# A recurrent mixing loop whose value rows are spread by DMA instead of by TensorE, with the orders of VectorE and ScalarE written out

## The chip, the cores and the metric

The kernel runs on one core of a Trainium2 chip. The core has TensorE (PE, matrix products, with its weight loads shown apart as PEld), VectorE (DVE), ScalarE (ACT), GpSimd (POOL) and SyncE (SP, which here only issues transfers). SBUF is the working memory of 128 partitions, PSUM the memory that TensorE writes to. Each engine has its own queue of instructions, and engines wait for each other by semaphores.

The metric is the device time of one execution in microseconds. The profile is taken from one execution of the program.

## The reference

Four layers run one after the other on an input of 8 batches, 256 rows and 512 channels, all in float32: a cross-attention layer with combined weights, a recurrent mixing layer, a pair of attentions with an MLP, and a non-local block. The change lies in the second layer. Cut to what matters, for each batch (S = 256 positions, 32 heads of 16 channels):

```
xa = layernorm(x); sx = shifted(xa) - xa
xw, xk, xv, xr, xg = xa + sx * (maa_* + low-rank mixes of xa and sx)
w = exp(-exp(time_decay + tanh(xw @ decay_w1) @ decay_w2))
r, k, v = xr @ Wr.T, xk @ Wk.T, xv @ Wv.T      # each head: 16 channels
g = silu(xg @ Wg.T)
for each position l, each head:
    a     = k_l[:, None] * v_l[None, :]         # 16 x 16
    out_l = r_l @ (faaaa * a + s)
    s     = a + w_l[:, None] * s
y = group_norm(out);  x = x + (y * g) @ Wo.T
xc = layernorm(x); sxc = shifted(xc) - xc       # channel mix
x = x + sigmoid(xr2 @ fWr.T) * (relu(xk2 @ fWk.T) ** 2 @ fWv.T)
```

The state of a head is 16 x 16 numbers, each of which follows a recurrence over the 256 positions: multiply by w of its row, add k of its row times v of its column.

## The kernel before

The program is written with a scheduling layer. Whatever is traced as an instruction carries its data dependences; a planner then orders the instructions of each engine by its own estimate of when they are ready, except where the program pins them. Two ways of pinning occur. `manual_schedule(engines=...)` keeps the named engines in the order of the program; `keep_in_program_order` does so for one instruction. The middle stage (class Middle, which holds the mixing layer and the two attentions) runs with PE pinned. DVE, ACT, POOL and SP are ordered by the planner there, apart from single pinned instructions.

**Layout.** Channels lie on partitions, 128 at a time (ct = 0 to 3), positions along the free dimension. For one batch, one ct and one half hf, a step of the loop handles 8 heads x 16 rows (128 partitions) x 8 value columns x 256 positions. So there are 8 x 4 x 2 = 64 steps, eight to a batch.

**One step** (functions spread, states and gather):

- `spread` (line 902): the value rows must stand on every partition of their head. Eight matmuls with a constant 0/1 matrix esel copy 32-partition groups of v to the PSUM tile vb (128 x 8 x 255). vb is 8 KB a partition, four of PSUM's eight banks, and has one buffer.
- `states`: on every second step ACT computes exp(-w) broadcast four times (w4, lines 912 and 913). DVE writes the initial state in column 0 of vb (line 921), multiplies vb by k in place in two halves (line 924), and runs two scans (line 928) over vb and w4. POOL multiplies each scan's result by r (line 933).
- `gather` (line 945): PE sums over the rows of the heads with the constant gsel into yp; on every second step DVE adds the bonus term hv (line 951).

**The filler.** All the rest of the layer is given as a list `steps + after` of (time, function): the projections k, v, r, g of a later batch, the mixes (`mixed`, line 777 on DVE), layernorms (`norm`, `normed`, `cm_norm`, `cm_normed`, `ln_stats` with its Ln and Exp on ACT at lines 60 and 61), the group norm (`head_norm`, `head_norm2`, `gated`, `gate`), `out_proj` and the channel mix (`cm_mix`, `cm_k`, `cm_r`, `cm_v`). The time is in steps; an item of batch b stands at 8 (b - 1) plus its time. So 19.1, the gate, falls on step 3.1 of a set of eight steps; 19.5, the output projection, on 3.5; 21, cm_norm, on 5.0; 7.1 is the second half of r. `fill.until(t)` traces all items up to t. Within a step the program traces: states(n), the filler up to n + 0.95, gather(n - 1), the filler up to n + 0.99 (the mixed items, which stand at .97), spread(n + 1). That order is PE's order.

**Banks.** Products of the filler go to PSUM tiles of tag mm, of which there are three during the loop. Most are emptied by ACT, those of mixed, bonus, out_proj, cm_v and partly g by DVE.

**Weights.** Eight weight matrices a batch pass through five buffers; each is loaded (line 1640, two transfers from SP) when the buffer's former user is behind it in the list. In the first layer's stage, which runs before with PE, DVE, ACT and POOL pinned, line 501 stores the result of a batch.

Of the kernel before, what the change touches and what calls it, by code (L numbers as in the profile page):

```python
# [10 lines left out]
F32 = mybir.dt.float32  # L11
AF = mybir.ActivationFunctionType
ALU = mybir.AluOpType
# [3 lines left out]
P = 128  # L17
B, S, D = 8, 256, 512
ST = S // P
CT = D // P  # L20
# [73 lines left out]
def rows_of(halves):  # L94

    return [halves[k // 2][:, k % 2, :] for k in range(CT)]
# [20 lines left out]
def stage_l0(g, pools):  # L117
# [492 lines left out]

    "bones": (P,), "bmean": (P,), "cmean": (P,),

    "esel": (4, P), "gsel": (4, 32),
    "bfa": (CT, P),
}
NMB, NMC = (
# [5 lines left out]
class Middle:  # L622
# [62 lines left out]
    def plan(self):  # L685
        g, cp, wpool = self.g, self.cp, self.wpool
        nc, I = g.nc, g.I
        HS, NG = 16, 4
        w1, w2, w2g, d1, d2, s0, bones, bmean, cmean, esel, gsel, bfa = self.c.values()

        class sm:
            tile = staticmethod(lambda *a, **k: self.sm.tile(*a, **k))
# [18 lines left out]
        bufs = [4]  # L711
# [6 lines left out]


        t_ = {}  # L720

        def fetch(b, tag, bufs):
            x = t_[tag, b] = wk.tile([P, ST, D], F32, tag=tag, name=tag, bufs=bufs)
            nc.sync.dma_start(out=x, in_=g.x1[b])

        def norm(b):
            t_["st", b] = ln_stats(g, sm, t_["xi", b])
# [79 lines left out]
                    nc.scalar.activation(w[:, ct, :], wp[:, j, :], AF.Exp, bias=g.pv("time_decay", ct))  # L807

        def load(b, W):
            t_[W, b] = rows_of(g.weight(wpool, I["l1" + W + "T"], name=W))  # L810

        def proj(b, W, src, c2):
            pp = mm("proj")
# [76 lines left out]
            nc.vector.tensor_tensor(xb[:, st, :], xb[:, st, :], op, ALU.add)  # L890


        vbs, rss, w4s, yps = {}, {}, {}, {}

        def spread(b, ct, hf):

            v_ = t_["v", b]
            vb = vbs[b, ct, hf] = ps.tile([P, NG, 2, S], F32, tag="vb", name="vb", bufs=1)
            for j in range(2):
                for n in range(NG):  # L900
                    r = slice(32 * n, 32 * n + 32)
                    nc.tensor.matmul(  # L902
                        vb[:, n, j, 1:S], lhsT=esel[r, 2 * hf + j, :], rhs=v_[r, ct, 0 : S - 1],
                        start=True, stop=True,
                    )

        def states(b, ct, hf):


            if hf == 0:  # L910
                w4 = w4s[b, ct] = wk.tile([P, 4, S], F32, tag="w4", name="w4")
                nc.scalar.memzero(w4[:, :, 0:1])
                nc.scalar.activation(
                    w4[:, :, 1:S], t_["w", b][:, ct : ct + 1, 0 : S - 1].to_broadcast([P, 4, S - 1]),
                    AF.Exp, scale=-1.0,
                )
            w4 = w4s[b, ct]
            kb = t_["k", b][:, ct : ct + 1, 0 : S - 1].to_broadcast([P, 4, S - 1])
            rb = t_["r", b][:, ct : ct + 1, :].to_broadcast([P, 4, S])
            vb = vbs.pop((b, ct, hf)).rearrange("p n j l -> p (n j) l")  # L920
            nc.vector.tensor_copy(vb[:, :, 0], s0[:, b, ct, hf])
            for n2 in range(2):
                h = vb[:, 4 * n2 : 4 * n2 + 4, 1:S]
                nc.vector.tensor_tensor(h, h, kb, ALU.mult)  # L924
            rss[b, ct, hf] = []
            for n2 in range(2):
                a = wk.tile([P, 4, S], F32, tag="a", name="a", bufs=6)
                nc.vector.tensor_tensor_scan(  # L928
                    a.rearrange("p n l -> p (n l)"), w4.rearrange("p n l -> p (n l)"),
                    vb[:, 4 * n2 : 4 * n2 + 4, :].rearrange("p n l -> p (n l)"), 0.0, ALU.mult, ALU.add,  # L930
                )
                rs = wk.tile([P, 4, S], F32, tag="a", name="rs", bufs=6)
                nc.gpsimd.tensor_tensor(rs, a, rb, ALU.mult)  # L933
                rss[b, ct, hf].append(rs)

        def gather(b, ct, hf):
            if hf == 0:
                yps[b, ct] = ps.tile([P, S], F32, tag="y", name="yp", bufs=1)
                if ct % 2 == 0:
                    t_["y", b, ct // 2] = wk.tile([P, 2, S], F32, tag="y", name="y", bufs=2)  # L940
            yp = yps[b, ct]
            rs2 = rss.pop((b, ct, hf))
            for j in range(2):
                for n in range(NG):
                    nc.tensor.matmul(
                        yp[32 * n : 32 * n + 32, :], lhsT=gsel[:, 2 * hf + j, :],
                        rhs=rs2[n // 2][:, 2 * (n % 2) + j, :],
                        start=(hf == 0 and j == 0), stop=(hf == 1 and j == 1),
                    )
            if hf == 1:  # L950
                nc.vector.tensor_tensor(
                    t_["y", b, ct // 2][:, ct % 2, :], yp, t_["hv", b][:, ct, :], ALU.add
                )
# [42 lines left out]

        def store(b):
            g.x2[b] = g.dram([P, ST, D], f"x2_{b}")
            nc.sync.dma_start(out=g.x2[b], in_=t_.pop(("xo", b)))


        HD, NH = 32, 4
        runs = [(pre, b) for pre in ("a_", "c_") for b in range(B)]

        pin = lambda ins: self.tc.keep_in_program_order(ins)

        def at_fetch(i):
            pre, b = runs[i]
# [170 lines left out]
        def values(i, ct):  # L1179
# [21 lines left out]
            (1.97, mixed, 0, *wk_), (2.97, mixed, 1, *wk_), (3.97, mixed, 0, *vr_), (4.97, mixed, 1, *vr_),  # L1201
            (5.97, mixed, 0, *g_), (6.97, mixed, 1, *g_),
            (4.2, decay), (4.1, kvrg, "k", 0), (5.2, decay2), (5.1, kvrg, "k", 1),
            (5.5, kvrg, "v", 0), (6.1, kvrg, "v", 1), (6.3, kvrg, "r", 0), (7.1, kvrg, "r", 1),
            (8.5, kvrg, "g", 0), (10.3, kvrg, "g", 1), (10.7, bonus),
            (13.4, head_norm, 0), (14.3, head_norm2, 0), (14.9, gated, 0), (15.8, gate, 0),
            (15, fetch, "xo", 2), (17.2, head_norm, 1), (18.05, head_norm2, 1), (18.6, gated, 1), (19.1, gate, 1),
# [18 lines left out]
        fill = self.fill = Filler()  # L1226
# [28 lines left out]
        for pre, i, q, kv, o in (("a_", 0, "w_qkv", "w_qkv", "w_ao"), ("c_", B, "w_q", "w_kv", "w_co")):  # L1255
            c = D if q == kv else 0
# [8 lines left out]
        for lo, hi, fn in spans:  # L1265
            free.sort()
            at = free.pop(0)
# [4 lines left out]
        def loop(psums):  # L1272
            every = [(b, ct, hf) for b in range(B) for ct in range(CT) for hf in range(2)]
            bufs[0] = 3
            fill.until(-0.001)
            spread(*every[0])
            for n, at in enumerate(every):
                states(*at)
                fill.until(n + 0.95)
                if n:  # L1280
                    gather(*every[n - 1])
                fill.until(n + 0.99)
                if n + 1 < len(every):
                    spread(*every[n + 1])
            gather(*every[-1])

            psums.close()
            self.ps = psums.enter_context(self.tc.tile_pool(name="atp", bufs=8, space=PSUM))
            bufs[0] = 8
            every = [(i, ct) for i in range(2 * B) for ct in range(CT)]  # L1290
            stream = [(i, ct, h2) for i, ct in every for h2 in range(2)]
            for n in range(-1, len(every)):
                fill.until(A0 + n + 0.05)
                if n + 1 < len(every):
                    scores(*every[n + 1])
                for k in (2 * n + 2, 2 * n + 3):
                    if k < len(stream):
                        masked(*stream[k])
                        exps(*stream[k])
                    if 0 < k <= len(stream):  # L1300
                        divided(*stream[k - 1])
                    if 1 < k:
                        turn(*stream[k - 2])
                fill.until(A0 + n + 0.95)
                if n > 1:
                    values(*every[n - 2])
                fill.until(A0 + n + 0.99)
            values(*every[-2])
            fill.until(A0 + len(every) + 0.99)
            values(*every[-1])  # L1310
            fill.until(999)
            psums.close()
            return t_["ln", 2 * B]
# [366 lines left out]
def host_layout(i):  # L1680

    f = np.float32
# [19 lines left out]
        a["l1" + nm + "T"] = T(L1[nm])  # L1702

    vo = np.arange(D).reshape(CT, 8, 16).transpose(0, 2, 1).reshape(-1)
    for nm in ("Wv", "Wg"):
        a["l1" + nm + "T"] = a["l1" + nm + "T"][:, vo]
    a["l1WoT"] = a["l1WoT"][vo]
    for nm in ("maa_w1", "decay_w1", "decay_w2"):
        a[nm] = L1[nm]
    w2 = L1["maa_w2"]  # L1710
    a["maa_w2p"], a["maa_w2g"] = w2[0:4].reshape(P, D), w2[4]

    a["sh"] = np.ascontiguousarray(c[:, 0:2].reshape(B, 2, CT, P).transpose(3, 1, 2, 0))

    s0 = c[:, 2:18].reshape(B, CT, P, 4, 2, 2).transpose(2, 0, 1, 4, 3, 5)
    a["s0"] = s0.reshape(P, B, CT, 2, 8)
    hs, th = np.arange(P) // 16, np.arange(P) % 8
    a["bones"] = (hs[:, None] == th[None, :]).astype(f)
    a["bmean"] = (th[:, None] == th[None, :]).astype(f) / 16
    a["cmean"] = np.eye(P, dtype=f) - a["bmean"]  # L1720
    t4 = np.arange(P) // 8 % 4
    a["esel"] = np.stack([((t4 == t)[:, None] & (th[:, None] == hs[None, :])) for t in range(4)], 1).astype(f)
    a["gsel"] = np.stack([((t4 == t)[None, :32] & (hs[:, None] == th[None, :32])) for t in range(4)], 1).astype(f)
    for nm in ("w_qkv", "w_ao", "w_q", "w_kv", "w_co", "w1", "w2"):
        a[nm] = L2[nm]
    a["thwT"] = T(L3["theta_w"])
# [1 line left out]
    a["wwT"] = T(L3["w_w"])  # L1728
    pv = {
        "gn_w": L1["gn_w"][vo], "gn_b": L1["gn_b"][vo],  # L1730
        "bo": L0["bo"], "rwb": L0["r_w_bias"], "faaaa": L1["faaaa"],
        "a_ln_s": L2["ln1_s"], "a_ln_b": L2["ln1_b"], "c_ln_s": L2["ln2_s"], "c_ln_b": L2["ln2_b"],
        "m_ln_s": L2["ln3_s"], "m_ln_b": L2["ln3_b"],
        "a_bq": L2["b_qkv"][0:D], "a_bk": L2["b_qkv"][D : 2 * D],
# [34 lines left out]
```

## Time and profile before

| what | us |
|---|---|
| median of 3 runs (3416.64 to 3420.81) | 3419.39 |
| the profiled execution | 3402.09 |
| its span in the profile | 3400.3 |
| mixing loop, first spread to last scan | 1375 to 2162 |

The profile's first part gives the busy time of each engine. Its rows by line give a group's count, its busy time, the mean of one in ns, and the idle time of the engine just before the group with what ended it. The table of stretches gives busy time per engine in a window and the mean granted clock of PE. The timeline lists instructions in order of time; in brackets stands how long the engine had been idle and what released it. "issue" is waiting for nothing that the profile shows.

### The profile page before, as it was taken

The numbers are of one execution on the slowest core, as the hardware profiler recorded it, in microseconds if no ns is written. First come the engines' busy times: TensorE is split into PE (matmuls) and PEld (weight loads), VectorE is DVE, ScalarE is ACT, GpSimd is POOL, SyncE is SP. The second block draws the span as 40 slices with busy tenths as digits, with TensorE's granted clock in tenths as the row PEclk, the third lists the DMA queues.
The fourth block names the chain that finished last, engine by engine and source line by source line (L and its number), as shares of the span: only waits on it lengthen the run. The fifth ranks groups of instructions, "written<-read, shape, count | busy, mean of one in ns | idle before, by whom it ended". The sixth has DMA issues, their size and how long they took to land. (4 is left out here: it accounts for less than half of the span.)

```text
span 3400.3 us, 68714 instructions
## 1 busy us (share of the span) xinstructions
PE 3186.7 (94%) x26496; PEld 2274.7 (67%) x26496; DVE 2408.6 (71%) x4175; ACT 1590.1 (47%) x3983; POOL 1663.7 (49%) x1776
## 2 busy tenths in 40 slices
PE   8999999999999997889999998899999997899999
PEld 6677777777777764656666655555555553799996
DVE  5666666666666664787787887667888886777771
ACT  4555555555555553224334333565656664323223
POOL 7533333333333232456656655443444443788872
PEclk9999999999999998889999999899999997999999
DMA  8666565656657542312323323267687776400002
GB/s 280 226 203 196 187 195 187 205 179 197 205 185 223 174 128 69 112 52 91 106 93 106 99 101 101 100 218 243 237 279 265 266 260 235 164 1 1 1 13 87
DMA packets 273141, 533.08 MB, mean 157 GB/s; under 512 B 25056, under 2 KB 147312, under 8 KB 268720
## 3 DMA queue, kind: packets, MB, share of 16 engines
q1 hardware_dynamic: 251616, 456.48, 41.6%
q10 hardware_dynamic: 20528, 70.39, 5.5%
q8 instruction: 211, 3.46, 0.4%
q0 software_dynamic: 672, 1.81, 0.2%
q14 instruction: 114, 0.93, 0.1%
HBM read 411.15 MB, written 117.44 MB: 155 GB/s over the span
## 5 line engine op out<-in xcount | busy, mean ns | idle before, releaser
L391 POOL TENSOR_SCALAR pe<-pe,rinv 128x512 f32<-128x512 f32 x256 | 176.9, 691 | 608.4 <-DVE rinv L390 605.8
L368 DVE TENSOR_REDUCE nmax<-sp 128x2 f32<-128x1024 f32 x256 | 309.1, 1217 | 176.6 <-PE sp L363 176.6
L933 POOL TENSOR_TENSOR rs<-a,r 128x1024 f32<-128x1024 f32 x128 | 302.7, 2380 | 254.4 <-DVE a L928 223.2
L1161 POOL TENSOR_SCALAR pe<-pe,rinv 128x256 f32<-128x256 f32 x512 | 235.3, 478 | 307.2 <-DVE rinv L1159 301.0
L377 ACT ACTIVATE pe<-sp,nmax 128x512 f32<-128x512 f32 x512 | 347.1, 683 | 11.2
L1151 ACT ACTIVATE pe<-pe,nmax 128x256 f32<-128x256 f32 x512 | 255.0, 499 | 200.5 <-DVE nmax L1142 197.7
L403 DVE STREAM_TRANSPOSE pt<-pe 128x1024 f32<-128x1024 f32 x256 | 312.8, 1231 | 24.2 <-POOL pe L391 15.3
L432 PE MATMUL av<-pt,vr 32*64 32x256 f32 x8192 | 263.8, 390 | 37.6 <-issue 28.9
L928 DVE TENSOR_TENSOR_SCAN a<-w,vb 128x1024 f32<-128x1024 f32 x128 | 287.4, 2276 | 4.8
L432 PEld LDWEIGHTS av<-pt,vr 32*64 32x64 f32 x8192 | 211.0, 136 | 102.8 <-issue 58.2
L363 PE MATMUL sp<-k,q 64*64 64x512 f32 x2048 | 265.8, 611 | 7.3 <-ACT pe L377 7.3
L373 ACT ACTIVATE nmax<-nmax 128x2 f32<-128x2 f32 x256 | 51.8, 202 | 397.8 <-DVE nmax L368 397.6
L303 PEld LDWEIGHTS gp<-t,ws 128*128 128x128 f32 x1512 | 184.8, 192 | 31.2 <-ACT pe L396 11.4
L303 PE MATMUL gp<-t,ws 128*128 128x128 f32 x1512 | 202.2, 277 | 2.5 <-POOL ws L289 1.4
L396 ACT ACTIVATE pe<-pe,rinv 128x512 f32<-128x512 f32 x256 | 182.6, 729 | 41.4 <-DVE rinv L390 41.4
L924 DVE TENSOR_TENSOR vb<-vb,k 128x1020 f32<-128x1020 f32 x128 | 157.2, 1228 | 4.4
L1171 DVE STREAM_TRANSPOSE dt<-pe 128x1024 f32<-128x1024 f32 x128 | 155.6, 1215 | 3.7 <-POOL pe L1161 3.7
L1447 ACT ACTIVATE h<-h,pvec 128x256 f32<-128x256 f32 x124 | 55.9, 500 | 201.6 <-DVE h L1416 164.6
L902 PE MATMUL vb<-v,mconstc 32*128 32x255 f32 x1024 | 98.9, 441 | 54.8 <-DVE a L928 54.0
L390 DVE RECIPROCAL rinv<-ssum 128x2 f32<-128x2 f32 x256 | 41.2, 161 | 146.8 <-ACT pe L377 146.8
L455 PEld LDWEIGHTS op<-av_sb,wo 128*128 128x128 f32 x512 | 92.2, 190 | 55.4 <-issue 27.5
L455 PE MATMUL op<-av_sb,wo 128*128 128x256 f32 x512 | 126.3, 390 | 2.1 <-issue 2.1
(311 smaller groups left out, 7537.7 us busy)
## 6 DMA issues: line engine op xcount, KB each, us to landing
pt<-dt ACTq DMA_DIRECT2D x128, 512.0 KB, 3.9
pt<-pt SPq DMA_DIRECT2D x512, 128.0 KB, 3.6
ws<-sqk SPq DMA_DIRECT2D x110, 512.0 KB, 4.8
wqk<-in_wqk_dram SPq DMA_DIRECT2D x70, 512.0 KB, 5.5
vr<-v SPq DMA_DIRECT2D x128, 256.0 KB, 4.7
ws<-sv SPq DMA_DIRECT2D x56, 512.0 KB, 4.9
wv<-in_wv_dram SPq DMA_DIRECT2D x36, 512.0 KB, 5.1
v<-vT SPq DMA_DIRECT2D x64, 256.0 KB, 2.5
```

Source lines behind the costliest of these rows:

```text
L303: nc.tensor.matmul(out[:, hf * P : (hf + 1) * P], lhsT=w[n](hf, k), rhs=a[n](hf, k), start=k == 0, stop=k == ST - 1,)
L363: nc.tensor.matmul(sp[a * 64 : (a + 1) * 64, h, :], lhsT=qs[b, 2 * un + a][r, ic], rhs=ks[b, 2 * un + a][r, :], start=True, stop=True,)
L368: nc.vector.tensor_reduce(nmax, sp, AX.X, ALU.max, negate=True)
L377: nc.scalar.activation(pe[:, h, :], sp[:, h, :], AF.Exp, bias=nmax[:, h : h + 1], scale=1.0 / DH ** 0.5, accum_out=ssum[:, h : h + 1],)
L396: nc.scalar.mul(pe[:, 1, :], pe[:, 1, :], rinv[:, 1:2])
L403: nc.vector.transpose(pts[b, un][:, it], pe)
L432: nc.tensor.matmul(av[r][h * DH : (h + 1) * DH], lhsT=vr[rows_, kb, h * DH : (h + 1) * DH], rhs=pt[rows_, :, h, 32 * kb : 32 * kb + 32], s ...
L455: nc.tensor.matmul(op, lhsT=wo[0][:, p % 4, mt * P : (mt + 1) * P], rhs=avs[b, p][:, c], start=p % 4 == 0, stop=p % 4 == 3,)
L928: nc.vector.tensor_tensor_scan(a.rearrange("p n l -> p (n l)"), w4.rearrange("p n l -> p (n l)"), vb[:, 4 * n2 : 4 * n2 + 4, :].rearrange( ...
L933: nc.gpsimd.tensor_tensor(rs, a, rb, ALU.mult)
L1151: pin(nc.scalar.activation(pe[:, r, :], pe[:, r, :], AF.Exp, bias=nmax[:, r : r + 1], scale=-1.0, accum_out=ssum[:, r : r + 1],))
L1161: pin(nc.gpsimd.tensor_scalar(pe[:, r, :], pe[:, r, :], rinv[:, r : r + 1], 1.0, ALU.mult, ALU.mult))
```

## The change

The value rows no longer pass through PE. v of a batch is stored to DRAM in two halves (`v_store`, at 5.8 and 6.45 in the list). For a step, `spread` issues eight transfers from DRAM to an SBUF tile vl (two buffers), one for each head residue h: the eight rows of a head's half are read 16 times, to the partitions h, h + 8, h + 16 and so on. `lift` copies vl to PSUM (vb) with two ScalarE copies of 128 x 1020 and, on every second step, computes w4. spread runs two steps ahead; lift(n + 1) is traced at n + 0.5.

In the loop, DVE and ACT join PE in the written order. The transfers of the loop (weights, fetches, stores, spreads) are pinned on SP. To let a head's rows lie at stride 8, the columns of Wr, Wk, the decay and faaaa are permuted on the host as those of v and g already were; esel is gone, and gsel, bones and s0 follow the new layout. The scratch for software DMA is set to 4096 bytes.

```diff
-            nc.sync.dma_start(out=x, in_=g.x1[b])
+            pin(nc.sync.dma_start(out=x, in_=g.x1[b]))
...
-            t_[W, b] = rows_of(g.weight(wpool, I["l1" + W + "T"], name=W))
+            t_[W, b] = rows_of(g.weight(wpool, I["l1" + W + "T"], name=W, pin=pin))
...
+        def v_store(b, c2):
+            if c2 == 0:
+                t_["vd", b] = g.dram([P, CT, S], f"v{b}")
+            c = slice(2 * c2, 2 * c2 + 2)
+            pin(nc.sync.dma_start(out=t_["vd", b][:, c, :], in_=t_["v", b][:, c, :]))
 
         def spread(b, ct, hf):
 
-            v_ = t_["v", b]
-            vb = vbs[b, ct, hf] = ps.tile([P, NG, 2, S], F32, tag="vb", name="vb", bufs=1)
-            for j in range(2):
-                for n in range(NG):
-                    r = slice(32 * n, 32 * n + 32)
-                    nc.tensor.matmul(
-                        vb[:, n, j, 1:S], lhsT=esel[r, 2 * hf + j, :], rhs=v_[r, ct, 0 : S - 1],
-                        start=True, stop=True,
-                    )
-
-        def states(b, ct, hf):
+            rows = t_["vd", b].rearrange("(g f h) c s -> h f c g s", f=2, h=2 * NG)
+            vl = vls[b, ct, hf] = wk.tile([P, 2 * NG, S], F32, tag="vl", name="vl", bufs=2)
+            for h in range(2 * NG):
+                pin(nc.sync.dma_start(
+                    out=vl[h :: 2 * NG, :, 1:S], in_=rows[h, hf, ct, :, 0 : S - 1].partition_broadcast(HS)
+                ))
+
+        def lift(b, ct, hf):
 
+            vl = vls.pop((b, ct, hf))
+            vb = vbs[b, ct, hf] = ps.tile([P, 2 * NG, S], F32, tag="vb", name="vb", bufs=1)
+            for n2 in range(2):
+                h = slice(NG * n2, NG * n2 + NG)
+                nc.scalar.copy(vb[:, h, 1:S], vl[:, h, 1:S])
             if hf == 0:
                 w4 = w4s[b, ct] = wk.tile([P, 4, S], F32, tag="w4", name="w4")
...
+            pin(nc.sync.dma_start(out=g.x2[b], in_=t_.pop(("xo", b))))
...
+            (5.5, kvrg, "v", 0), (6.1, kvrg, "v", 1), (5.8, v_store, 0), (6.45, v_store, 1), (6.3, kvrg, "r", 0), (7.1, kvrg, "r", 1),
...
+            fill.until(-1.45)
+            spread(*every[0])
+            spread(*every[1])
             fill.until(-0.001)
-            spread(*every[0])
-            for n, at in enumerate(every):
-                states(*at)
-                fill.until(n + 0.95)
-                if n:
-                    gather(*every[n - 1])
-                fill.until(n + 0.99)
-                if n + 1 < len(every):
-                    spread(*every[n + 1])
+            lift(*every[0])
+            with self.tc.manual_schedule(engines={getattr(mybir.EngineType, e) for e in ("PE", "DVE", "Activation")}):
+                for n, at in enumerate(every):
+                    states(*at)
+                    if n + 2 < len(every):
+                        spread(*every[n + 2])
+                    fill.until(n + 0.5)
+                    if n + 1 < len(every):
+                        lift(*every[n + 1])
+                    fill.until(n + 0.95)
+                    if n:
+                        gather(*every[n - 1])
+                    fill.until(n + 0.99)
             gather(*every[-1])
...
-    for nm in ("Wv", "Wg"):
+    for nm in ("Wr", "Wk", "Wv", "Wg"):
         a["l1" + nm + "T"] = a["l1" + nm + "T"][:, vo]
...
-    nc = _bacc.Bacc("TRN2", target_bir_lowering=False, num_devices=1)
+    nc = _bacc.Bacc("TRN2", target_bir_lowering=False, num_devices=1, dynamic_dma_scratch_size=4096)
```

More of the change, by code (lines that the diff above doesn't have):

```diff
@@ L611 @@
     "bones": (P,), "bmean": (P,), "cmean": (P,),
-    "esel": (4, P), "gsel": (4, 32),
+    "gsel": (4, 32),
     "bfa": (CT, P),
@@ L688, in plan @@
         HS, NG = 16, 4
-        w1, w2, w2g, d1, d2, s0, bones, bmean, cmean, esel, gsel, bfa = self.c.values()
+        w1, w2, w2g, d1, d2, s0, bones, bmean, cmean, gsel, bfa = self.c.values()
         class sm:
@@ L720, in plan @@
         t_ = {}
+        pin = lambda ins: self.tc.keep_in_program_order(ins)
         def fetch(b, tag, bufs):
             x = t_[tag, b] = wk.tile([P, ST, D], F32, tag=tag, name=tag, bufs=bufs)
-            nc.sync.dma_start(out=x, in_=g.x1[b])
+            pin(nc.sync.dma_start(out=x, in_=g.x1[b]))
         def norm(b):
@@ L890, in out_proj @@
             nc.vector.tensor_tensor(xb[:, st, :], xb[:, st, :], op, ALU.add)
-        vbs, rss, w4s, yps = {}, {}, {}, {}
-        def spread(b, ct, hf):
-            v_ = t_["v", b]
-            vb = vbs[b, ct, hf] = ps.tile([P, NG, 2, S], F32, tag="vb", name="vb", bufs=1)
-            for j in range(2):
-                for n in range(NG):
-                    r = slice(32 * n, 32 * n + 32)
-                    nc.tensor.matmul(
-                        vb[:, n, j, 1:S], lhsT=esel[r, 2 * hf + j, :], rhs=v_[r, ct, 0 : S - 1],
-                        start=True, stop=True,
-                    )
-        def states(b, ct, hf):
+        vls, vbs, rss, w4s, yps = {}, {}, {}, {}, {}
+        def v_store(b, c2):
[3 more added lines that the diff above has]
+            pin(nc.sync.dma_start(out=t_["vd", b][:, c, :], in_=t_["v", b][:, c, :]))
+        def spread(b, ct, hf):
+            rows = t_["vd", b].rearrange("(g f h) c s -> h f c g s", f=2, h=2 * NG)
[10 more added lines that the diff above has]
+                nc.scalar.copy(vb[:, h, 1:S], vl[:, h, 1:S])
             if hf == 0:
@@ L916, in states @@
                 )
+        def states(b, ct, hf):
             w4 = w4s[b, ct]
@@ L919, in states @@
             rb = t_["r", b][:, ct : ct + 1, :].to_broadcast([P, 4, S])
-            vb = vbs.pop((b, ct, hf)).rearrange("p n j l -> p (n j) l")
+            vb = vbs.pop((b, ct, hf))
             nc.vector.tensor_copy(vb[:, :, 0], s0[:, b, ct, hf])
             for n2 in range(2):
-                h = vb[:, 4 * n2 : 4 * n2 + 4, 1:S]
+                h = vb[:, NG * n2 : NG * n2 + NG, 1:S]
                 nc.vector.tensor_tensor(h, h, kb, ALU.mult)
@@ L929, in states @@
                     a.rearrange("p n l -> p (n l)"), w4.rearrange("p n l -> p (n l)"),
-                    vb[:, 4 * n2 : 4 * n2 + 4, :].rearrange("p n l -> p (n l)"), 0.0, ALU.mult, ALU.add,
+                    vb[:, NG * n2 : NG * n2 + NG, :].rearrange("p n l -> p (n l)"), 0.0, ALU.mult, ALU.add,
                 )
@@ L945, in gather @@
                     nc.tensor.matmul(
-                        yp[32 * n : 32 * n + 32, :], lhsT=gsel[:, 2 * hf + j, :],
+                        yp[32 * n : 32 * n + 32, :], lhsT=gsel[:, 2 * j + hf, :],
                         rhs=rs2[n // 2][:, 2 * (n % 2) + j, :],
@@ L998, in store @@
             g.x2[b] = g.dram([P, ST, D], f"x2_{b}")
-            nc.sync.dma_start(out=g.x2[b], in_=t_.pop(("xo", b)))
+            pin(nc.sync.dma_start(out=g.x2[b], in_=t_.pop(("xo", b))))
         HD, NH = 32, 4
         runs = [(pre, b) for pre in ("a_", "c_") for b in range(B)]
-        pin = lambda ins: self.tc.keep_in_program_order(ins)
         def at_fetch(i):
@@ L1203, in plan @@
             (4.2, decay), (4.1, kvrg, "k", 0), (5.2, decay2), (5.1, kvrg, "k", 1),
-            (5.5, kvrg, "v", 0), (6.1, kvrg, "v", 1), (6.3, kvrg, "r", 0), (7.1, kvrg, "r", 1),
+            (5.5, kvrg, "v", 0), (6.1, kvrg, "v", 1), (5.8, v_store, 0), (6.45, v_store, 1), (6.3, kvrg, "r", 0), (7.1, kvrg, "r", 1),
             (8.5, kvrg, "g", 0), (10.3, kvrg, "g", 1), (10.7, bonus),
@@ L1709, in host_layout @@
         a[nm] = L1[nm]
+    a["decay_w2"] = a["decay_w2"][:, vo]
     w2 = L1["maa_w2"]
@@ L1713, in host_layout @@
     a["sh"] = np.ascontiguousarray(c[:, 0:2].reshape(B, 2, CT, P).transpose(3, 1, 2, 0))
-    s0 = c[:, 2:18].reshape(B, CT, P, 4, 2, 2).transpose(2, 0, 1, 4, 3, 5)
+    s0 = c[:, 2:18].reshape(B, CT, 8, 16, 4, 2, 2).transpose(3, 2, 0, 1, 6, 4, 5)
     a["s0"] = s0.reshape(P, B, CT, 2, 8)
-    hs, th = np.arange(P) // 16, np.arange(P) % 8
-    a["bones"] = (hs[:, None] == th[None, :]).astype(f)
+    th = np.arange(P) % 8
+    a["bones"] = (th[:, None] == th[None, :]).astype(f)
     a["bmean"] = (th[:, None] == th[None, :]).astype(f) / 16
@@ L1721, in host_layout @@
     t4 = np.arange(P) // 8 % 4
-    a["esel"] = np.stack([((t4 == t)[:, None] & (th[:, None] == hs[None, :])) for t in range(4)], 1).astype(f)
-    a["gsel"] = np.stack([((t4 == t)[None, :32] & (hs[:, None] == th[None, :32])) for t in range(4)], 1).astype(f)
+    a["gsel"] = np.stack([((t4 == t)[None, :32] & (th[:, None] == th[None, :32])) for t in range(4)], 1).astype(f)
     for nm in ("w_qkv", "w_ao", "w_q", "w_kv", "w_co", "w1", "w2"):
@@ L1730, in host_layout @@
         "gn_w": L1["gn_w"][vo], "gn_b": L1["gn_b"][vo],
-        "bo": L0["bo"], "rwb": L0["r_w_bias"], "faaaa": L1["faaaa"],
+        "bo": L0["bo"], "rwb": L0["r_w_bias"], "faaaa": L1["faaaa"].reshape(-1)[vo], "time_decay": L1["time_decay"][vo],
         "a_ln_s": L2["ln1_s"], "a_ln_b": L2["ln1_b"], "c_ln_s": L2["ln2_s"], "c_ln_b": L2["ln2_b"],
```

## The prediction

> **What bounds the kernel now.** The page's busy line and its rows name the engines of the whole run; a table by stretches then picks out the mixing loop (1375 to 2162 us), the only stage that the change touches; the timeline gives its order.
>
> ```profile
> PE 3186.7 (94%) x26496; PEld 2274.7 (67%) x26496; DVE 2408.6 (71%) x4175; ACT 1590.1 (47%) x3983; POOL 1663.7 (49%) x1776
> ...
> L902 PE MATMUL vb<-v,mconstc 32*128 32x255 f32 x1024 | 98.9, 441 | 54.8 <-DVE a L928 54.0
> ```
> The spread matmuls (L902) keep PE busy for 98.9 us, 1.55 us a step over 64 steps.
>
> ```profile
> 1571.00:1669.00 98.00, 93.83 (x561) 60.81 (x560) 80.62 (x90) 36.70 (x68) 61.58 (x29) 0.98 0.29 97
> 1669.00:1767.00 98.00, 93.82 (x555) 60.19 (x554) 79.95 (x90) 36.37 (x68) 62.17 (x29) 0.97 0.31 103
> ...
> 1375.00:2162.00 787.00, 718.25 (x4288) 469.29 (x4286) 635.02 (x683) 282.06 (x508) 471.60 (x222) 0.95 0.27 89
> ```
> Columns: stretch, length, busy PE, PEld, DVE, ACT, POOL, clock, DMA share, GB/s. In the steady part PE is busy 96% of the time, DVE 82%, ACT 37%. PE bounds it, DVE is close behind.
>
> ```profile
> 1563.47 0.17 DVE L921 COPY vb<-mconstc 128x8 f32<-128x8 f32 x1 [1.35 <-PE vb L902]
> ...
> 1864.70 0.17 DVE L921 COPY vb<-mconstc 128x8 f32<-128x8 f32 x1 [1.35 <-PE vb L902]
> ```
> These open steps 16 and 40: 301.2 us for three sets of eight steps, 100.4 us a set. Sets 0 and 1 (1376.9 to 1563.5) took 93.3 each.
>
> ```profile
> 1795.05 1.15 DVE L876 SCALAR_TENSOR_TENSOR g<-g,y 128x512 f32<-128x512 f32 x1 [0.41 <-ACT y L869]
> ...
> 1801.68 0.16 DVE L921 COPY vb<-mconstc 128x8 f32<-128x8 f32 x1
> ...
> 1804.39 7.03 PE L881 MATMUL projs<-Wo,g 128*128 128x512 f32 x16
> ...
> 1810.14 0.69 DVE L58 BATCH_NORM_STATS2 ln_stats<-xo 128x6 f32<-128x512 f32 x1
> ...
> 1827.17 0.16 DVE L921 COPY vb<-mconstc 128x8 f32<-128x8 f32 x1
> ```
> Step 3 opens at 1801.68 and step 5 at 1827.17. The gate (step list 3.1) ran before step 3's states, and cm_norm's statistics (list 5.0) began 17 us before step 5. The planner had moved DVE's work ahead of its place in the program. That is what the reader has to see: the step list was good for PE's order alone.
>
> **The change, part by part.** Steps are counted within a set (0 to 7); "states" is copy 0.16, two products 2.49, two scans 4.46: 7.1 us of DVE.
>
> *Removed:* eight spread matmuls a step, 8 x 1.55 = 12.4 us of PE a set. PE's 96% of 100.4 is 96.4; about 1.5 of the spread ran beside the mixed matmuls, so 85 us remain.
>
> *Added transfers:* 64 a set on SP, each 16 x 8 rows of 1020 B. The nearest row is attention's 128 KB load of 128 rows of 1 KB:
> ```profile
> L1177 SPq DMA_DIRECT2D pt<-pt x512: 577/602/1582, 2184.4 to 2882.3; - x171
> ...
> DMA to landing us min/median/max: 2.5/3.7/8.7
> ```
> Eight issues at 0.6 are 4.8 us, the last lands 3.7 later: 8.5 us (7.1 to 21.4 by both ends). They are issued about 1.5 steps ahead, some 18 us; SP's other 21 transfers a set cost it 8 us at 0.37 each. Hidden by that lead; at the far end they would be 3 us late, which is a rival below. SP is now in program order, so a weight load that waits for PE also holds the spreads behind it, but the work it waits for lies in the step before, so I cost that at nothing. The value store (two a set, 2.6 us to landing as the x<-xo store) is hidden by the same lead. [...]
>
> *Added copies:* two of 128x1020 on ACT a step. ACT writes no PSUM in this trace; the Exp of that shape (L913) takes 1.04 us, twice the 128x512 PSUM read of L377 (0.683) is 1.37. I take 1.04, same shape: 16.6 us a set on an engine busy 37%; 1.37 would lengthen one wait below by 0.7. The copies wait for the last scan of the step before (vb has one buffer), and ACT's queue waits with them.
>
> *Order:* this decides. After each of steps 1 to 6 the mixed matmuls end PE's step and DVE must evacuate them before the next states. So DVE begins states 0.6 (wait) + 1.6 (four products) = 2.2 us after PE ended the step (1.5 after steps 5 and 6, two products), and everything listed later waits 7.1 us more. PE has three banks of tag mm; ACT empties most of them, in order. Five places follow:
>
> - Step 5: cm_norm is listed first. Its Ln waits for DVE: 2.2 + 7.1 + statistics 1.6; Ln and Exp with two table loads of 1.28 are 3.1; only then comes k's copy, 0.6. Total 14.6. PE has by then done k 3.7 and decay2 2.0 in its three banks and waits: 8.9 us.
> - Step 3: out_proj needs the gate behind states: 2.2 + 7.1 + 0.7 = 10.0, while PE has only cm_v, 3.7: 6.3 us.
> - Step 7 to 0: norm's Ln and Exp end at 1.5 + 7.1 + 1.6 + 3.1 = 13.3, its normalising at 14.7; PE, done at 12.0, waits 2.7 for the transposes' input. ACT then has r's copy 0.6, cm_k 1.2, the lift 2.1, the w4 exponential 1.25 and cm_r's Tanh 0.6: the bank is free at 19.1, PE wants it at 15.9: 3.2 us.
> - Step 0 to 1: shift now follows the g product, which waits for PE's g (26.4): Tanh 0.6, product 0.7, subtraction 1.2 and four products of 0.46 to 0.99. lora ends about 2.6 us late.
> - Steps 2 and 6: banks held by mixed (1.2) and behind the lift (1.7): 2.9 us.
>
> Sum of waits 26.6. A wait of this length also lowers the clock; the row nearest:
> ```profile
> 2160.00:2180.00 20.00, 12.75 (x71) 7.14 (x72) 12.66 (x33) 6.52 (x24) 6.47 (x6) 0.53 0.00 0
> ```
> With 7 of 20 us idle the clock was 0.53; steady stretches have 0.98. In the steady loop the trace's clock record has half-speed spells of 3.4 or 6.8 us, about one a set; each costs half its length: between 0 (none longer than today) and four of 6.8 (13.6 us); I take 5, one short spell for each of the three longest waits. [...]
>
> A full set becomes 85 + 26.6 + 5 = 117 us, 17 more than 100.4.
>
> *Start:* weight loads are pinned too. Today:
> ```profile
> 1292.05 4.66 SPq L1640 DMA_DIRECT2D Wk<-in_l1WkT_dram  x2
> ...
> 1353.32 0.34 SPq L501 DMA_DIRECT2D x<-x  x1
> ```
> The last store of the first layer (L501) now stands ahead of Wk. Wk then lands near 1358 and k begins 9.5 us after its 1348.8. From v's last copy (1369.5) to the first product (1377.1) are 7.6 us today; store 3.0, eight loads 8.5 and a copy 1.0 make 12.5, 4.9 more: together 14 us.
>
> *Small ones at nothing:* esel's load is gone (early, beside the first layer); smaller scratch for software DMA (constants only); relabelled columns (same shapes).
>
> *Sum* against the profiled execution (3402.1 us, span 3400.3): start +14; set 0, without the older batch's work, 0; set 1, now full, 117 - 95 = +22; sets 2 to 6, 5 x 17 = +85; set 7, without mixed and its coupling, +5. That is +126: 3528. The median of the runs shown is 17.3 above the profiled execution: **3545**.
>
> **Rivals.**
> *Faster: VectorE as the bound, 3384.* If the queues absorb the waits, a set falls to DVE's 82.5 us plus eight lift gaps of 1.2 between scan and product, 92: six sets x -8.4 + 15 = -35. For it: DVE has 18% to spare now. Against: it decides only where the waits stay under 100.4 - 85 - 2.5 (the start's share) = 13 a set, and steps 5 and 3 alone make 15. 7%.
> *The orders are not in force, 3370:* the planner keeps arranging DVE and ACT; PE's 85 and today's 4 to 5 us of PE idle leave about 90 a set: 6 x -10.4 + 14 = -48. Against: PE's order under the same block is the program's today. 4%, with 1% for a result between.
> *Milder, 3465:* an engine's lag spreads over several steps and half of the waits overlap: 126 - 6 x 13.3 = +46. For it: DVE's waits in one step give ACT time to catch up for the next. Against: the mixed matmuls tie the engines together at the end of six steps of eight. 16%.
> *Transfers late, 3690:* 1020 B rows from DRAM repeated 16 times are slower than the row above, or SP's waits hold them; 3 us in 48 steps adds 145. Against: DMA share 0.3 here, and 0.7 to 0.8 in attention without a late page. 8%.
>
> **How the numbers follow.** The forecast, waits of about the size worked out, has 64%, and lies between 3500 (no clock loss, -30, and waits a tenth smaller, -16) and 3650 (four spells of 6.8, +52, and waits a third larger, +53). Its own range is that. With the milder case down to 3430 the range 3430 to 3650 holds 80%; the two faster cases (11%), the late transfers (8%) and 1% lie outside. 0.2% (7 us) is about what can be told from no change: faster 0.11, same 0.01, slower 0.88.
>
> **What would show it.** L902 gone, PE's busy time down by about 99; ACT rows vb<-vl near 1.04 us, x128; SP issues vl x512 near 0.6. Right: a set of about 117 us; PE idle on ACT for proj or yc in step 5 of some 9 us and on DVE's gate ahead of projs<-Wo of some 6; clock below 0.95 in the loop; Wk issued after L501. Wrong: PE waits under 13 us a set, DVE busy over 88% in the loop; ACT's copies waiting for DMA vl would mean late transfers; statistics of cm_norm ahead of states would mean that the orders do not hold.

## The result and the profile after

The changed kernel takes 3517.14 us (median; 3511.20 to 3520.83) against 3418.01 (3415.90 to 3420.81) for the kernel before: a ratio of 1.0289 (1.0274 to 1.0304), slower by 99 us. The forecast was 3545, with a range of 3500 to 3650.

The page of the kernel after, its busy line and the row of the new copies:

```profile
PE 3166.8 (90%) x25472; PEld 2249.4 (64%) x25472; DVE 2398.2 (68%) x4175; ACT 1726.4 (49%) x4121; POOL 1663.6 (47%) x1775
...
L917 ACT COPY vb<-vl 128x1020 f32<-128x1020 f32 x128 | 129.7, 1013 | 144.9 <-DVE a L940 100.8
```
The 1024 spread matmuls are gone from PE, 98.9 us of them, and yet its busy time fell by 20 only. ACT has the 128 copies at 1.01 us. Most of ACT's idle time before them ends with VectorE's scan (a), not with a transfer (33.1 us, eight lifts).

Next the stretches of two full sets, from first states to first states (columns as in the prediction):

```profile
1717.30:1833.30 116.00, 93.89 (x440) 59.62 (x440) 80.48 (x91) 55.47 (x88) 61.82 (x29) 0.90 0.60 163
1833.30:1949.40 116.10, 93.92 (x440) 59.62 (x440) 80.53 (x92) 55.54 (x89) 61.82 (x29) 0.90 0.63 163
```
A set takes 116 us where it took 100.4. No engine is the bound any more: PE is busy 94 us, DVE 80, ACT 55, and PE has 22 us of idle time in every set. The waits of PE over the five full sets (1601.5 to 2181.8) say whom it waits for; columns: total, times, longest.

```profile
PE yc L853 <- ACT k L834: 37.2, 5, 8.5
PE projs L882 <- DVE g L877: 22.1, 5, 4.4
PE ln_tp L83 <- DVE xn L68: 14.7, 4, 3.7
PE proj L818 <- ACT th L1001: 12.5, 5, 3.1
PE tp L754 <- DVE xxx L745: 10.8, 5, 2.2
PE projs L882 <- DVE x_maa_w L778: 6.9, 5, 1.4
PE proj L818 <- DVE x_maa_g L778: 4.8, 5, 1.0
```
109.0 us, 21.8 a set. In the kernel before, PE's only large wait in the loop was that of the spread for the scan, 16.3 us in five sets and never above 2.5. The timeline shows the two longest, step 3's and step 5's, in the set from 1833.30:

```profile
1869.52 0.16 DVE L933 COPY vb<-mconstc 128x8 f32<-128x8 f32 x1
...
1876.68 0.94 DVE L877 SCALAR_TENSOR_TENSOR g<-g,y 128x512 f32<-128x512 f32 x1
1877.68 6.90 PE L882 MATMUL projs<-Wo,g 128*128 128x512 f32 x12 [4.42 <-DVE g L877]
...
1899.47 0.16 DVE L933 COPY vb<-mconstc 128x8 f32<-128x8 f32 x1
...
1906.57 0.67 DVE L58 BATCH_NORM_STATS2 ln_stats<-xo 128x6 f32<-128x512 f32 x1
...
1908.28 0.29 ACT L60 ACTIVATE ln_rstd<-ln_mv,eps 128x2 f32<-128x2 f32 x1 [9.36 <-DVE ln_mv L59]
1910.00 0.57 ACT L834 COPY k<-proj 128x512 f32<-128x512 f32 x1
1910.62 2.08 PE L853 MATMUL yc<-y,mconstc 128*128 128x512 f32 x2 [7.19 <-ACT k L834]
```
The gate now stands behind step 3's states, which open at 1869.52 and hold DVE for 7.1 us; the output projection waits for it. In step 5, cm_norm's statistics stand behind the states of 1899.47, ACT's Ln waits 9.36 us for them, and k's copy, which needs nothing of cm_norm, waits on ACT's queue behind the Ln. PE gets its bank 7.19 us late. In the kernel before, gate and statistics had both run ahead of the states.

The start, from the timeline:

```profile
1363.21 0.34 SPq L501 DMA_DIRECT2D x<-x  x1
1363.60 0.43 SPq L1657 DMA_DIRECT2D Wk<-in_l1WkT_dram  x1
...
1368.29 4.73 PE L818 MATMUL proj<-x_maa_k,Wk 128*128 128x256 f32 x12 [7.48 <-DMA Wk<-in_l1WkT_dram]
...
1401.50 0.17 DVE L933 COPY vb<-mconstc 128x8 f32<-128x8 f32 x1 [22.03 <-ACT vb L917]
```
The second half of Wk is issued after the first layer's last store (L501), and PE waits 7.48 us for it. From that store to the first states are 38.3 us, against 23.6 before: 14.7 more. The store itself came 9.9 us later than in the trace of before, in a stage where both programs are the same; over the runs here it lay between 1353.3 and 1366.5. Behind the loop, where both are the same again, the trace of after is 7.2 us longer (1250.6 against 1243.4; 1238 to 1251 over the runs). The stages that the change touches, start and loop, hold 14.7 and 86.9: 101.6 of the 118.8 us between the two traces, close to the 99 of the medians.

### The profile page after: what moved, and what is told of

Its sections match the earlier page's. It is cut to its first block, busy times and chain, and to the rows that moved or that the text cites. A ratio compares the mean times of both kernels' runs of the same rounds, so it can differ in the third digit from the quotient of the medians.

```text
span 3519.1 us, 67621 instructions
## 1 busy us (share of the span) xinstructions
PE 3166.8 (90%) x25472; PEld 2249.4 (64%) x25472; DVE 2398.2 (68%) x4175; ACT 1726.4 (49%) x4121; POOL 1663.6 (47%) x1775
## 5 line engine op out<-in xcount | busy, mean ns | idle before, releaser
L403 DVE STREAM_TRANSPOSE pt<-pe 128x1024 f32<-128x1024 f32 x256 | 312.7, 1231 | 24.2 <-POOL pe L391 15.3
L432 PE MATMUL av<-pt,vr 32*64 32x256 f32 x8192 | 271.0, 397 | 39.5 <-issue 31.4
L917 ACT COPY vb<-vl 128x1020 f32<-128x1020 f32 x128 | 129.7, 1013 | 144.9 <-DVE a L940 100.8
```

Of the source, the lines that this page charges most:

```text
L403: nc.vector.transpose(pts[b, un][:, it], pe)
L432: nc.tensor.matmul(av[r][h * DH : (h + 1) * DH], lhsT=vr[rows_, kb, h * DH : (h + 1) * DH], rhs=pt[rows_, :, h, 32 * kb : 32 * kb + 32], s ...
```

## The experiments

The theory was the prediction's: in the written order, work that PE waits for stands behind 7.1 us of states on DVE, or behind such a wait on ACT, and PE has too few banks to run on. Its rivals: transfers or the clock make the sets long; or the transfers' path (SP, the copies) matters more than the orders. In each experiment "loop" is the time from the first states to the last, 780.0 us before and 866.9 after. Every ratio is to the kernel before, run beside it on the same chip.

### One wait moved: cm_norm a fiftieth of a step earlier

```diff
-            (21, cm_norm), (21.6, cm_normed), (21.9, cm_norm_T), (22, cm_mix),
+            (20.98, cm_norm), (21.6, cm_normed), (21.9, cm_norm_T), (22, cm_mix),
```

> cm_norm stands at 20.98 instead of 21 in the list, so that DVE's statistics come ahead of step 5's states and ACT's Ln no longer holds k's copy until they end. Theory (queues in written order): the wait of yc on ACT k, 7.4 us a set, goes; about 1.4 us comes back because cm_normed now ends after the transposes want it; with a shorter half-speed spell (1 to 2 us) a full set falls from 116.1 to 108 to 110, six sets and a part of set 7, so 36 to 55 us less than the changed kernel: 3462 to 3481. Rival (the engines are tied elsewhere too, the wait only moves on): under 15 us, above 3500.

3487.84 us, ratio 1.0237 (1.0200 to 1.0273), by the ratios about 18 us better than the changed kernel; in the traces the loop took 842.7, 24.2 shorter. Step 5 fell from 21.6 to 15.8 us. PE's waits in its five full sets (1592.5 to 2160.6):

```profile
PE projs L882 <- DVE g L877: 22.1, 5, 4.4
PE proj L818 <- ACT th L1001: 15.6, 5, 3.1
PE ln_tp L83 <- DVE cn L68: 14.1, 9, 2.1
```
The wait for k, 37.2 us, is gone but for 0.9; the gate's is untouched. That tells the site of the theory from the rivals: a list entry that touches no transfer takes the longest wait away. Less was gained than the 36 us expected at least: PE now waits for cn, the normalised input of the transposes, 14.1 us in all, and its busy time rose to 98.1 us a set, as 19.6 us of it a set (13.4 in the changed kernel) fell into half-speed spells of the clock record.

### The other long wait: the gate before step 3's states

```diff
-            ... (18.6, gated, 1), (19.1, gate, 1),
+            ... (18.6, gated, 1), (18.98, gate, 1),
```

> The gate of the second half stands at 18.98 instead of 19.1, ahead of step 3's states. Theory (written order): the wait of projs<-Wo on DVE g, 4.4 us on PE and 5.3 on its weight loads, goes, and the short half-speed spell behind it: a set falls by 5 to 6.5 us, in all 30 to 42 us: 3475 to 3487. Rival (the wait moves on to the mixed items at the end of the step, whose banks DVE empties late): under 10 us, above 3507.

3480.53 us, ratio 1.0225 (1.0175 to 1.0275), by the ratios about 22 us better; the loop 838.2, 28.7 shorter, just short of what was expected. The wait for the gate is gone from PE's list, step 3 fell from 18.7 to 10.8 us, and the wait for k stayed at 37.2. The gate's own product, in the timeline, took 2.42 us here and 0.94 in the changed kernel:

```profile
1843.78 2.42 DVE L877 SCALAR_TENSOR_TENSOR g<-g,y 128x512 f32<-128x512 f32 x1
```
It had moved beside GpSimd's products. This comes back below.

### The planner's orders given back to DVE and ACT

```diff
-            with self.tc.manual_schedule(engines={getattr(mybir.EngineType, e) for e in ("PE", "DVE", "Activation")}):
+            with self.tc.manual_schedule(engines={getattr(mybir.EngineType, e) for e in ("PE",)}):
```

> The changed kernel with PE alone in written order in the loop; DVE and ACT are left to the planner again, the transfers, copies and pins stay. Theory (the written orders cost the time, the transfers are hidden): a set of 90 to 96 us, against 116 as changed and 100.4 before; with the start's 15 us that is 3370 to 3410, faster than before or the same. Rival (transfers, ACT's copies or the pinned SP queue cost the time): stays within 25 us of the changed kernel, above 3490.

4206.96 us, ratio 1.2347 (1.2304 to 1.2390): sets of 208 us. Every expectation missed. The waits of all engines over two sets (1800 to 2216):

```profile
POOL rs L945 <- DVE a L940: 200.5, 16, 16.7
...
PE yp L957 <- POOL rs L945: 173.3, 33, 13.1
DVE vb L933 <- ACT vb L917: 77.5, 12, 11.6
ACT k L834 <- PE proj L818: 61.7, 4, 19.1
```
PE waits in the gather for POOL, POOL for the scan, the scan's step for ACT's lift, and ACT stands up to 19.1 us in front of work that needs PE's next products. As these rows read, the planner placed the lift behind such work, in a circle with PE's written order; no run pinned the lift alone. No wait for a spread transfer is among them. So with the lift on ScalarE this planner's orders cost far more than the written ones: these are a remedy inside the change, and the prediction's price for "the orders are not in force" (3370) was wrong by over 800 us.

### The written orders alone, spread still on PE

The kernel before with its loop wrapped as in the change:

```diff
+            with self.tc.manual_schedule(engines={getattr(mybir.EngineType, e) for e in ("PE", "DVE", "Activation")}):
-            for n, at in enumerate(every):
+                for n, at in enumerate(every):
...
```

> The kernel before, spread on PE, with DVE and ACT put in written order in the loop and nothing else. Theory: PE's 97 us with the spread, 18 to 22 us of the same waits and 4 to 5 us of clock make a set of about 120 us against 100.4: 3520 to 3560. Rival (the transfers cost the time, the orders nothing): 3410 to 3430.

3471.03 us, ratio 1.0186 (1.0143 to 1.0228); the loop 843.1, sets 112.6. PE's waits (1582.2 to 2145.4):

```profile
PE yc L852 <- ACT k L833: 32.0, 5, 6.4
PE projs L881 <- DVE g L876: 17.9, 5, 3.6
PE tp L753 <- DVE xxx L744: 9.1, 5, 2.1
PE vb L902 <- DVE a L928: 8.8, 5, 1.8
```
The first three are sites of the changed kernel, in the same order, with no transfer and no lift in the program; the fourth is the spread's own. The orders alone cost 63.1 us of loop, where the whole change costs 86.9. With the rest of the change PE has less to do (busy 94 us a set against 99), and the waits for xn and for cm_r's Tanh (th), which stands behind the lift, are added; what each part of that rest costs was not measured alone. A set was expected near 120 and grew by 12 us in place of 20, so the time lies below the 3520 expected at least, though far above the rival.

### Loads left to the planner

```diff
-            t_[W, b] = rows_of(g.weight(wpool, I["l1" + W + "T"], name=W, pin=pin))
+            t_[W, b] = rows_of(g.weight(wpool, I["l1" + W + "T"], name=W))
```

> The changed kernel with the weight loads of the mixing layer left to the planner on SP, as before; spreads, stores and fetches stay pinned. Theory: only the start gains, Wk being issued ahead of the first layer's last store: 6 to 10 us less, ratio 1.025 to 1.028, the loop within 5 us of 866.9. Rival (SP's written order holds the spreads up in the loop): the loop falls by 15 us or more.

3497.06 us, ratio 1.0279 (1.0236 to 1.0322). From the last store to the first states it took 30.9 us in place of 38.3: the 7.4 us are PE's wait for Wk (7.48), as expected. In the profiled execution the loop grew by 12 to 879.3, with 29.2 us a set at half speed in the clock record, and more than the gain was lost again. But that execution is the longest of the four, 3521.68; the three others, 3492.24 to 3499.71, lie 8 to 15 us below the changed kernel by their ratios, as much as the start's gain or more. Whether the loop pays for this order of the loads is not settled. The rival, a loop shorter by 15 us, did not show.

### One transfer in place of eight

```diff
-            for h in range(2 * NG):
-                pin(nc.sync.dma_start(
-                    out=vl[h :: 2 * NG, :, 1:S], in_=rows[h, hf, ct, :, 0 : S - 1].partition_broadcast(HS)
-                ))
+            pin(nc.sync.dma_start(
+                out=vl[:, :, 1:S], in_=t_["vd", b][:, ct : ct + 1, 0 : S - 1].to_broadcast([P, 2 * NG, S - 1])
+            ))
```

> The changed kernel with one transfer of 128 partitions x 8 rows of 1020 B in place of eight of 16 partitions; each partition gets its own row eight times, so the values are not spread over the head. Theory (transfers are hidden behind the lead of two steps): the loop within 5 us of 866.9, at the start 3 to 5 us less; ratio 1.025 to 1.030. Rival (eight issues a step on SP or the repeated reads hold ACT's copies): the loop falls by 15 us or more.

3502.04 us, ratio 1.0279 (1.0255 to 1.0302). Its stretches of the same two sets:

```profile
1716.50:1832.50 116.00, 93.84 (x440) 59.57 (x440) 80.44 (x91) 55.47 (x88) 61.83 (x29) 0.90 0.56 163
1832.50:1948.60 116.10, 93.84 (x440) 59.54 (x440) 80.52 (x92) 55.55 (x89) 61.82 (x29) 0.90 0.54 163
```
The same to 0.1 us. The transfers, first in the changed kernel, then here:

```profile
L907 SPq DMA_DIRECT2D vl<-v x512: 532/598/2027, 1388.6 to 2242.6; - x171
...
DMA to landing us min/median/max: 3.1/4.4/9.7
```
```profile
L906 SPq DMA_DIRECT2D vl<-v x64: 359/367/938, 1387.8 to 2228.0; - x64
...
DMA to landing us min/median/max: 7.2/9.2/16.5
```
One big transfer lands 9.2 us (median) after its issue, eight small ones take 4.8 us of issuing and 4.4 more, which is the same. In the middle of the loop both are hidden by the lead of a step and a half. Its end is an exception: the last full set took 111.1 us here and 116.4 in the changed kernel, where one lift waited 7.3 us for its transfer, and the set behind it 82.7 and 86.6, with a wait of 3.0. So the loop is 8.5 us shorter here (858.4), more than the 5 allowed for.

### All five waits moved, with and without transfers

The list of the changed kernel with every late item ahead of the states that held it:

```diff
-            (-3.9, fetch, "xi", 1), (-1, norm), (-0.4, normed), (0.2, norm_T), (0.5, shift), (1.1, lora),
+            (-3.9, fetch, "xi", 1), (-1.3, norm), (-1.02, normed), (0.2, norm_T), (0.45, shift), (1.1, lora),
...
-            ... (19.1, gate, 1),
+            ... (18.98, gate, 1),
...
-            (21, cm_norm), (21.6, cm_normed), (21.9, cm_norm_T), (22, cm_mix),
+            (19.85, cm_norm), (20.98, cm_normed), (21.9, cm_norm_T), (22, cm_mix),
```

> The changed kernel with seven times in the list moved so that DVE's and ACT's short work stands ahead of the states that it waited behind: cm_norm 19.85 and cm_normed 20.98 (from 21 and 21.6), the second gate 18.98, norm -1.3 and normed -1.02 (from -1 and -0.4), shift 0.45 (from 0.5, ahead of the g product). Theory: of PE's 22.6 us of waits a set some 4 stay; with less half-speed time a set is 95 to 99 us against 116.1 (before: 100.4), the loop from first to last states 740 to 765 us against 866.9 (before 780.0), the ratio to the kernel before 0.990 to 1.004. Rival (the waits move on, as part of cm_norm's did): a set above 106, ratio above 1.015.

3411.36 us, ratio 1.0011 (0.9997 to 1.0025): no difference from the kernel before. The loop fell by 97 us to 769.9, sets to 100 to 102.4, a little above what was expected. PE's waits (1586 to 2091) are led by one that grew, for cm_r's Tanh. The Tanh stands behind the lift and the lift waits for a scan, which comes late because DVE had waited 7.4 us for the norm's Ln and Exp:

```profile
PE proj L818 <- ACT th L1001: 33.7, 5, 6.7
PE projs L882 <- DVE x_maa_w L778: 9.5, 5, 2.0
```

The same moves and orders in the kernel before (spread on PE; the edit is the two diffs above put together):

> The kernel before, spread on PE, with DVE and ACT in written order and the same seven moves. Theory: PE's 97 us with the spread, some 3 us of waits and 2 to 4 of clock: a set of 101 to 105 us, loop 785 to 815 (orders alone: 843.1), ratio 1.000 to 1.012; the run with all moves and the transfers is 4 to 8 us a set shorter. Rival (the moves help only by the transfers): loop above 835.

3393.19 us, ratio 0.9950 (0.9933 to 0.9967); the loop 770.7, shorter than expected. The two loops differ by 1 us, where 4 to 8 us a set had been expected in favour of the transfers; the transfers' longer start (39.2 us from the last store to the first states, against 23.7) then makes up most of the 18 us between the two times.

A last pair moves the norm further ahead, to -2.05 and its normalising to -1.4, first in the kernel with transfers (whose first loads were left unpinned as well):

> The run with all moves and the transfers, with norm and normed a step earlier still (-2.05 and -1.4 in place of -1.3 and -1.02), because there DVE waited 7.4 us a set for norm's Ln and Exp, which stood behind ACT's other work, and PE 6.7 us for cm_r's bank behind the late lift; the first batch's weight loads alone are unpinned. Theory: both waits go, a set falls from 100.6 to 93 to 97 us, the loop from 769.9 to 725 to 750, the start by 7: ratio to the kernel before 0.983 to 0.994. Rival (DVE, busy 85.7 of 100.9 us a set, is already the bound): a set above 99, ratio above 0.997.

3386.74 us, ratio 0.9916 (0.9893 to 0.9939), the loop 749.5, both as expected, though a full set took 96.8 to 100.7, not 93 to 97. Then with the spread on PE:

> The run with all moves and the spread on PE, with the same earlier norm. PE is busy 96 of 101.4 us a set there, so the theory gives at most 2 to 4 us a set: 97.5 to 99.5 us, loop 745 to 760, ratio 0.987 to 0.994; if PE's work is the bound, it is then 2 to 5 us a set longer than the same with transfers. Rival (the waits were off the path): loop within 5 us of 770.7, ratio about 0.995.

3377.70 us, ratio 0.9898 (0.9876 to 0.9919), the loop 749.9, as expected, but a set is 0.5 us longer than with transfers, not 2 to 5. It is the fastest of all, 1% below the kernel before. From the first layer's last store to the first states it needs 23.4 us, the version with transfers 29.5.

So with PE relieved by the transfers the loop is as long as without. Stretches of a set each say why, first two of the kernel with transfers, then one with the spread on PE:

```profile
1661.40:1758.30 96.90, 88.99 (x440) 56.95 (x440) 88.01 (x92) 55.93 (x90) 64.13 (x30) 0.98 0.70 197
1758.30:1856.50 98.20, 92.14 (x440) 58.64 (x440) 87.94 (x92) 55.70 (x89) 64.08 (x30) 0.95 0.70 193
```
```profile
1755.90:1854.90 99.00, 95.25 (x570) 62.50 (x571) 89.78 (x92) 40.23 (x71) 63.79 (x29) 0.98 0.31 101
```
DVE, with the same instructions, went from 80.5 to 87.9 and 89.8 us. Its further idle time in the version with transfers is mainly the lift (waits of DVE, 1563.2 to 2055.4):

```profile
DVE vb L933 <- ACT vb L917: 29.6, 16, 4.3
```
That is 5.9 a set: 87.9 + 5.9 = 93.8 of 98.2. The other candidate is PE, busy 92.1 of 98.2. But in the first of the two sets, with less time at half speed, PE had 3.2 us less to do, and the set was only 1.3 us shorter. As these sums read, VectorE and its coupling to the copies have become the bound, and the time that PE was spared is not used; no run tested that by itself. Where DVE's extra 7 to 9 us come from is in the last part.

## Why the prediction was right, and where it was off

**Direction and mechanism: right.** All five places named were found, the two largest in their order (step 5's k, step 3's gate). A set was put at 117 us and took 116.1.

**That sum holds by two misses that cancel.** Waits were put at 26.6 us and measured 22.1 of idle time: for k 7.2 (8.9 forecast), for the gate 4.4 (6.3), norm 3.7 (2.7), cm_r's bank 2.4 (3.2), xxx 2.2 (2.6), the two small bank waits 1.4 and 1.0 (1.2 and 1.7; the second too ended with a mixed item, not with the lift). The wait for k is shorter mostly by the table load of the Ln, 1.28 us, which ACT did before the statistics were there (it stands at 1897.64, the Ln at 1908.28); the working had it behind them. The wait for the gate is shorter as four matmuls of the output projection (1.88 us at 1871.38) ran ahead of the wait. On the other side, "about 1.5 of the spread ran beside the mixed matmuls, so 85 us remain" was mis-sized. The rows of the loop's PE groups add up to 104.2 us a set before and its busy time to 96.3, so 7.8 overlapped; after, 97.2 and 93.9, 3.3. Removing 12.5 us of spread so saved about 8.0, not 11. The other groups grew by 5.4, half-speed matmuls among them: 96.4 - 8.0 + 5.4 = 93.8 busy.

**Clock: right in size, in part by luck.** In the clock record 4.8 us a set ran at half speed before, 23.1 after, in three spells (10.2, 10.2 and 3.4); with PE busy in 4.5 and 13.4 of them, the loss rose from 2.25 to 6.7, by 4.5 (5 forecast). The forecast took three short spells of 3.4 and half of their length. Two of the three were 10.2 long, and by half of their length the loss would have risen by 9; it did not because PE stood idle in 9.7 of the 23.1 us. The longest waits of PE have a spell at them, with a granted clock of 0.50 in each. In the changed kernel the three spells of a set lie at its three longest waits (7.2, 4.4 and 3.7 us): 1904.6 to 1914.8, 1877.3 to 1880.7 and 1945.6 to 1955.8 in the set shown. In the kernel before, from 2070 on, waits of 7.74, 4.34 and 6.24 us, which end at 2084.8, 2122.4 and 2164.4, have spells from 2079.5, 2120.4 and 2161.4. How long a wait has to be for this the runs do not show: the wait for k began at 1903.4, only 1.2 us ahead of its spell; before the change no wait of PE in the full sets is longer than 2.5 us, and each of that length has a spell of 3.4 or 6.8 us at it; in the last version with transfers none is longer than 2.7, and 8.9 us a set ran at half speed.

**Start: right,** 14.7 against 14. Its parts: the wait for Wk was 7.5 (9.5), and from v's last copy to the first product there were 13.5 us (12.5).

**Sets at the edges: too high, and this is most of the miss.** Set 0 was put at 0 and got 3.2 us shorter; set 1 at +22, measured +16.7 (113.3); set 7 at +5, measured -4.4; sets 2 to 6 at +85, measured +78. For sets 0 and 7 the saved spread is the likely reason; no run shows it alone. Start and loop together: 101.7 in place of 126. These 24 us are the gap between 3545 and 3517, but for 4: 3402.1 + 17.3 + 101.7 = 3521.

**Transfers hidden: right for nearly all,** with landing at 4.4 us for the 3.7 of the row used, and copies of 1.01 for 1.04. Eight lifts of the 64 waited for a transfer, 33.1 us in all. Sets of the same length with one transfer in place of eight say that these did not count, but for the two at the loop's end.

**Rivals.** "VectorE as the bound, 3384" did not come about under this list, but with the waits moved the kernel with transfers came to 3387, and as the sums above read it is bounded as that rival had it, by a DVE that is 5 us a set busier than it was put at and lift gaps smaller than the 9.6 it allowed. That the times agree is luck: the rival put a full set at 92 and it took 98.4, and shorter sets at the edges made up for it. "The orders are not in force, 3370" was the wrong way round: 4207. "Milder, 3465" let half of the waits overlap, and 22.1 of 26.6 us stayed. "Transfers late, 3690" put 3 us on 48 steps, and only the eight lifts above waited.

## What to carry to other kernels

Here work taken off the busiest engine bought nothing, as the order on the other engines did not let it run on. Before such a change, read what stands in each in-order queue between a producer and the waiting engine, and price it by the instructions ahead of it. When an order is taken from a planner and written by hand, look in the trace for what the planner had run earlier than the list says, and move these entries first. Here that was worth 97 us of loop with the transfers and 72 without them, and the transfers themselves nothing. Measure the parts apart: the written order with the moved entries, without the transfers, was the fastest version.

## What the runs showed of the hardware that was not expected

**VectorE slower beside GpSimd.** The two normalising products of cm_norm, in the timeline of the changed kernel (GpSimd idle from 1909.3 to 1922.9):

```profile
1910.13 1.00 DVE L68 TENSOR_SCALAR cn<-xo,ln_mv,ln_rstd 128x512 f32<-128x512 f32 x2 [1.88 <-ACT ln_rstd L61]
```
and in the fastest version, with GpSimd's products beside them:

```profile
1817.90 2.17 POOL L784 TENSOR_TENSOR x_maa_v<-x_maa_v,xs 128x1024 f32<-128x1024 f32 x1
1818.18 4.49 DVE L68 TENSOR_SCALAR cn<-xo,ln_mv,ln_rstd 128x512 f32<-128x512 f32 x2
1820.03 2.36 POOL L784 TENSOR_TENSOR x_maa_r<-x_maa_r,xs 128x1024 f32<-128x1024 f32 x1
...
1822.60 0.15 DVE L921 COPY vb<-mconstc 128x8 f32<-128x8 f32 x1
```
1.00 us became 4.49, and the pair ends at 1822.68, 0.29 us behind GpSimd's product (1822.39). xn's pair went from 1.00 to 3.93 in the same way, xxx's four products from 1.67 to 3.64 and the gate's from 0.94 to 2.10: together 9.5 us, all of the 9.3 that DVE is busier in a set (80.5 to 89.8). DVE's products that read PSUM (L777, 0.47 us) took the same in both. Of the products named here (cn, xn, xxx and the gate, between 1400 and 2100 us) 43 of 62 were lengthened by more than a quarter in the fastest version, 19 of 62 in the kernel before and 5 of 61 in the changed one. Every one of them ended 0.28 to 0.29 or 0.55 us behind an instruction of GpSimd, and none of the others lay wholly beside one. Why they end there no row shows, and no run here moved GpSimd's products away to test it. Moving DVE's work earlier had a price here, as it then lay beside GpSimd's products: the 9.5 us above.

**Half-speed spells move.** A group of 16 matmuls that takes 3.72 us at full speed (L818 at 1897.79), in the changed kernel begun within the spell of 1829.5 to 1839.7, behind a wait of 2.35 us:

```profile
1834.89 6.11 PE L818 MATMUL proj<-fmaa_k,fWk 128*128 128x256 f32 x16 [2.35 <-ACT th L1001]
```
With cm_norm earlier the longest wait was gone and the half-speed time with PE busy rose, from 13.4 to 19.6 us a set; in the profiled execution with the loads left to the planner it was 20.0. Which idle pattern opens a spell is not settled by these runs.
